# Four halo buffers instead of two, and the next image's plan entered first, in a four-layer image kernel on one core

## The chip, the cores and the metric

The kernel runs on one core of a Trainium2 chip. The metric is the device time of one execution in microseconds. A program is run several times and the median is taken; beside that one execution is profiled, and all durations below come from it.

## The reference

A batch of four images of 64 x 64 pixels with 96 channels passes through four layers. The change lies in the first two, both selective scans over an image (4096 tokens) in four directions:

```
x   -> normalise over groups of channels -> in_proj: 96 -> 192 (inner) and 192 (gate z)
inner -> depthwise 3x3 convolution -> SiLU -> x_tok          gate z -> SiLU -> z_t
for each of 4 directions k (token orders):
    dt, B, C = projections of x_tok[order k]
    h_t = exp(dt*A) * h_(t-1) + dt*x_t*B_t ;  y_k[t] = C_t . h_t
sum over k of weight_k * y_k, brought back to image order, + D * x_tok
-> layer norm -> * z_t -> (layer 0: out_proj 192 -> 96, + x)
```

Layer 0 has diagonal and radial orders, and weights for the four directions that depend on the pixel. Layer 1 has rows and columns, forwards and backwards, and plain sums, and its output goes on into a convolutional feed-forward part. Layers 2 and 3 (attention, FFN, Fourier layers) follow and are not touched.

## The kernel before

Class Stream runs both scan layers as eight batches, one per layer and image, in one order written out by hand (`run`). Each batch is 4 directions x 4 segments of 1024 tokens. A segment is a run of slots in which DVE scans (line 918), POOL multiplies by C (line 928), ACT makes the decays (line 906) and PE spreads and gathers (lines 898 and 939). These stretches are the bulk of the time and are the same in both kernels.

Between two batches stands `side_by_side`. It interleaves two works that don't depend on each other:

- `front(bt)` prepares the batch after the next: it loads the image in four strips of 16 rows (`measure`, line 368, tile da), takes statistics on DVE (line 372), and loads for each strip the row above and the row below (`edges`, line 380, tile halo). `project` clears the border of a padded buffer (line 415, tile spare, two buffers), normalises the strip and its halo rows on DVE (line 420), and multiplies by the input weights on PE (line 428 for the inner half, 444 for the gate), with ACT writing into the padded buffer (line 434) and making z (line 447). `convolve` runs the 3x3 convolution of the strip on PE out of the padded buffer (line 481), SiLU on ACT (493), and transposes (502, 505) into x_tok (514).
- `merge(bt)` ends the batch before: in eight chunks of 512 tokens it loads x_tok (line 557, tile dx, one buffer), multiplies it by D on POOL (565 in layer 0, 568 in layer 1), adds the four directions on DVE (610 in layer 0, 614 in layer 1), where the last two of layer 0 are gathered by POOL's indirect DMAs (587, tile h, four buffers), takes layer-norm statistics (624), and in `finish` normalises (637), transposes on PE into one PSUM buffer u (645), scales on ACT (655), multiplies by z on DVE (659), projects on PE (671) and adds x (676).

At the first boundary `side_by_side` has two fronts and no merge. The six boundaries after that have one front and one merge (four merge layer 0, two merge layer 1), the next has only a merge, and the last stands behind the whole scan.

The order of instructions is decided at build time by a planner, class Plan. Each work is a generator that yields an engine and a cost in microseconds before it emits instructions, or a condition to wait for. The planner always takes the thread with the earliest start, and of equal ones the one with the larger `ahead`, then the one that was entered first:

```
start = max(th.at, self.free.get(th.wants[0], 0.0))
if best is None or (start, -th.ahead) < (best[0], -best[1].ahead):
    best = start, th
```

Fronts are entered with ahead = 1 and merges with 0; threads that a thread enters inherit its value. Buffers of limited number are taken from rings (`take`, `give`): a thread that wants a buffer waits in the plan until another has given one back. `give` counts from the moment at which the using instruction is put into the program, not from its end on the chip; the semaphores that hold the instruction until the buffer is really free are set by the framework. On the chip each engine's instructions run in the order that the planner made. All loads and stores named here are issued by one queue, SP, in that same order.

The halo of a strip is given back at the end of `project`, after the gate's projection:

```
yield from plan.together([outer(j) for j in range(2)])
give(st.x, st.halo)
```

Of the kernel before, what the change touches and what calls it, by code (L numbers as in the profile page):

```python
# [22 lines left out]
HW = 64  # L23
L = HW * HW
C = 96
# [175 lines left out]
class Rings:  # L201
# [9 lines left out]
    def take(self, pool, shape, tag, bufs, dtype=F32):  # L211
        ring = self.rings.setdefault(tag, SimpleNamespace(busy=[False] * bufs, at=0, tiles=None))
        while ring.busy[ring.at]:
            yield lambda: not ring.busy[ring.at]
        slot, ring.at = ring.at, (ring.at + 1) % bufs
        ring.busy[slot] = True
        x = ring.tiles[slot] if ring.tiles else self.k.t(pool, shape, tag, dtype, bufs=bufs)
        self.slots[id(x)] = ring, slot, x
        return x
# [92 lines left out]
class Stream:  # L312
# [38 lines left out]
    def front(self, bt, plan, rings, first=None):  # L351

        k, nc, lay = self.k, self.nc, bt.lay
        take, give = rings.take, rings.give
# [18 lines left out]

        def edges(s, st):

            halo = yield from take(self.tmp, [C, 2, HW], "halo", 2)
            yield "SP", 0.1
            for n, row in enumerate((s * 16 - 1, s * 16 + 16)):
                if 0 <= row < HW:
                    nc.sync.dma_start(halo[:, n], x[:, row * HW : (row + 1) * HW])  # L380
            yield "none", 2.5
            st.halo = halo

        for s, st in enumerate(strips):
            plan.add(edges(s, st))
# [300 lines left out]
    def side_by_side(self, ahead, behind=None, flush=None, seg=None):  # L686


        k, nc = self.k, self.nc
        plan, rings = Plan(), Rings(k)  # L690
        self.ended, self.idle = False, None

        def ending():

            yield "none", 1.2
            if flush:
                flush()
            self.idle = k.t(self.ps_y, [128, CH], "y")
            self.ended = True
            yield "PE", 4.0  # L700

        def fill():
            if self.idle is not None:
                data = self.layers[0].diag.rearrange("p h t c -> p (h t c)")[:, :384]
                nc.tensor.matmul(self.idle[:GC, :384], self.zeros, data, start=True, stop=True)

        def states():

            for at in range(2 * NSG):
                yield "none", 50.0 if at == 0 else 4.0  # L710
                yield "SP", 0.1
                self.load_states(seg, *divmod(at, NSG))
            self.load_dt(seg, 0)

        plan.fill = fill
        if seg:
            plan.add(states())
        if behind:
            plan.add(self.merge(behind, plan, rings))
        for bt in ahead:  # L720
            plan.add(self.front(bt, plan, rings, None if bt is ahead[0] else ahead[0]), 1)
        plan.add(ending())
        plan.run()
        self.idle = None
# [1386 lines left out]
```

## Time and profile before

| | |
|---|---|
| median of 3 runs | 15879.18 us (15832.05 to 15962.23) |
| profiled execution | 15861.73 us |
| its span, first to last instruction | 15859.9 us |
| granted TensorE clock, mean | 0.875 |
| DVE busy | 12867.0 us (81%) |
| POOL busy | 9781.6 us (62%) |
| ACT busy | 8291.1 us (52%) |

The first page of the profile gives busy times and a strip of 40 slices for each engine. A group or timeline line names the time, the duration, the engine, the source line (L), the operation, the tile written and the tile read, the shape, and in square brackets how long the engine was idle before it and what ended that. Tile names leave out the number of the buffer. "SPq" is the issue of a DMA on SP; the data land some microseconds later.

### The profile page before, as it was taken

The numbers are of one execution on the slowest core, as the hardware profiler recorded it, in microseconds if no ns is written. First come the engines' busy times: TensorE is split into PE (matmuls) and PEld (weight loads), VectorE is DVE, ScalarE is ACT, GpSimd is POOL, SyncE is SP. The second block draws the span as 40 slices with busy tenths as digits, with TensorE's granted clock in tenths as the row PEclk, the third lists the DMA queues.
The fourth block names the chain that finished last, engine by engine and source line by source line (L and its number), as shares of the span: only waits on it lengthen the run. The fifth ranks groups of instructions, "written<-read, shape, count | busy, mean of one in ns | idle before, by whom it ended". The sixth has DMA issues, their size and how long they took to land. (4 is left out here: it accounts for less than half of the span.)

```text
span 15859.9 us, 190275 instructions
## 1 busy us (share of the span) xinstructions
PE 13616.6 (86%) x70721; PEld 4897.8 (31%) x70721; DVE 12867.0 (81%) x9642; ACT 8291.1 (52%) x14188; POOL 9781.6 (62%) x4913
## 2 busy tenths in 40 slices
PE   7888888888888888888888888888888889998877
PEld 3222322232223222322222223222222234443344
DVE  1989798979897989799979997999899965665555
ACT  3656465556565655556655655656556522332333
POOL 0788688867886788677757775777677730000223
PEclk8888888888898888888888888888888899998888
DMA  2333433343334333433343334333433310000132
GB/s 71 110 103 121 153 108 104 120 152 106 104 122 153 106 103 120 154 109 115 113 150 118 108 118 147 111 122 116 141 118 108 115 53 18 18 11 14 46 75 70
DMA packets 662747, 1637.10 MB, mean 103 GB/s; under 512 B 102822, under 2 KB 268459, under 8 KB 658044
## 3 DMA queue, kind: packets, MB, share of 16 engines
q1 hardware_dynamic: 624956, 1549.37, 30.9%
q0 software_dynamic: 36864, 75.55, 1.6%
q8 instruction: 560, 9.18, 0.2%
q14 instruction: 367, 3.01, 0.1%
HBM read 1295.03 MB, written 329.58 MB: 102 GB/s over the span
## 5 line engine op out<-in xcount | busy, mean ns | idle before, releaser
L928 POOL TENSOR_TENSOR hc<-h,bc 128x1024 f32<-128x1024 f32 x3072 | 7186.7, 2359 | 2360.7 <-DVE h L918 1949.8
L918 DVE TENSOR_TENSOR_SCAN h<-da,state,t 128x1024 f32<-128x1024 f32 x2304 | 5271.5, 2329 | 11.5 <-ACT da L906 8.7
L939 PE MATMUL y<-hc,gather_y 128*32 128x512 f32 x12288 | 4270.8, 687 | 628.4 <-POOL hc L928 465.1
L911 DVE TENSOR_TENSOR t<-u,bc 128x1024 f32<-128x1024 f32 x3072 | 3601.2, 1218 | 895.2 <-PE u L898 780.8
L906 ACT ACTIVATE da<-dts,L_A_logs 128x1024 f32<-128x1024 f32 x3072 | 3488.0, 1147 | 726.7 <-DMA dts<-dt_dram 444.4
L898 PE MATMUL u<-dtu,spread 32*128 32x512 f32 x3072 | 1879.7, 739 | 369.4 <-DVE t L911 362.9
L962 PE MATMUL y<-L_diag,zeros 96*32 96x256 f32 x5218 | 1736.9, 463 | 0.0
L918 DVE TENSOR_TENSOR_SCAN h<-da,t 128x1024 f32<-128x1024 f32 x768 | 1711.0, 2269 | 13.1 <-ACT da L906 12.5
L939 PEld LDWEIGHTS y<-hc,gather_y 128*32 128x32 f32 x12288 | 800.1, 117 | 2404.0 <-issue 1210.4
L830 PE MATMUL m<-xs,proj 96*128 96x512 f32 (+1 forms) x2048 | 1018.3, 620 | 121.8 <-ACT dt L839 62.7
L867 ACT COPY dt<-m 96x512 f32<-96x512 f32 x512 | 297.1, 580 | 1458.9 <-PE m L862 1458.9
L898 PEld LDWEIGHTS u<-dtu,spread 32*128 32x128 f32 x3072 | 595.1, 214 | 1433.1 <-issue 1117.5
L962 PEld LDWEIGHTS y<-L_diag,zeros 96*32 96x32 f32 x5218 | 617.2, 132 | 1274.9 <-issue 1114.7
L1289 POOL MEMSET padp<- 128x2448 f32 x32 | 68.6, 2143 | 1396.7 <-PE d L1329 1375.5
L1365 DVE SCALAR_TENSOR_TENSOR hcv<-padv,taps,hcv 128x2048 f32<-128x2048 f32 x384 | 902.2, 2350 | 13.4
L1329 PE MATMUL d<-padp,diag 32*32 32x512 f32 x25600 | 885.5, 601 | 2.0 <-ACT hcp L1344 2.0
L822 POOL TENSOR_TENSOR dtu<-sp_z,dtu 96x1024 f32<-96x1024 f32 x256 | 604.4, 2361 | 384.7 <-ACT dtu L820 382.3
L862 PE MATMUL m<-sp_z,ident 96*96 96x512 f32 x1024 | 537.1, 606 | 195.6 <-ACT sp_z L856 195.6
L834 ACT ACTIVATE sp_z<-m,L_dtb 96x512 f32<-96x512 f32 x512 | 349.3, 682 | 540.4 <-PE m L830 531.6
L1329 PEld LDWEIGHTS d<-padp,diag 32*32 32x32 f32 x25600 | 483.4, 103 | 370.6 <-issue 197.7
L986 ACT COPY spare<-m 128x512 f32<-128x512 f32 x384 | 225.6, 587 | 711.0 <-PE m L983 710.8
L830 PEld LDWEIGHTS m<-xs,proj 96*128 96x128 f32 (+1 forms) x2048 | 322.4, 177 | 829.4 <-issue 325.8
(275 smaller groups left out, 15623.6 us busy)
## 6 DMA issues: line engine op xcount, KB each, us to landing
bc<-bc_dram SPq DMA_DIRECT2D x1024, 512.0 KB
dts<-dt_dram SPq DMA_DIRECT2D x768, 512.0 KB
dt_dram<-dt SPq DMA_DIRECT2D x256, 384.0 KB
y_tok<-spare SPq DMA_DIRECT2D x64, 768.0 KB
dt<-y_tok SPq DMA_DIRECT2D x128, 384.0 KB
x_tok<-y_rows SPq DMA_DIRECT2D x32, 768.0 KB
z_t<-z_rows SPq DMA_DIRECT2D x64, 384.0 KB
dx<-x_tok SPq DMA_DIRECT2D x64, 384.0 KB
```

Of the source, the lines that this page charges most:

```text
L822: rest = lambda half: nc.gpsimd.tensor_add(r[:, half], z[:, half], r[:, half])
L830: nc.tensor.matmul(ps, proj[:, src, to], xs[:, src, cols], start=src == 0, stop=src == 1)
L862: nc.tensor.matmul(ps, k.ident[:C, :C], term[:, half, cols], start=at == 0, stop=at == 2)
L898: self.nc.tensor.matmul(seg.u[:, cols], self.spread[rows, :], seg.dtu[rows, half, cols], start=True, stop=True)
L906: self.nc.scalar.activation(da, seg.dts[cb], AF.Exp, scale=seg.bt.lay.neg_a[:, seg.kd, g : g + 1])
L911: self.nc.vector.tensor_mul(gr.t, gr.seg.u, self.bc[:, 0, gr.sg, :])
L918: self.nc.vector.tensor_tensor_scan(gr.h[:, order], gr.da[:, order], gr.t[:, order], start, op0=ALU.mult, op1=ALU.add)
L928: self.nc.gpsimd.tensor_mul(gr.hc, gr.h, self.bc[:, 1, gr.sg, :])
L939: nc.tensor.matmul(seg.y[at : at + GC, :], self.gather_y, gr.hc[:, part * CH : (part + 1) * CH], start=gr.sg == 0, stop=gr.sg == NSG - 1, ...
L962: self.nc.tensor.matmul(gr.seg.y[at : at + GC, :256], self.zeros, gr.seg.bt.lay.diag.rearrange("p h t c -> p (h t c)")[:, :256], start=Fal ...
L1329: nc.tensor.matmul(pc[i][j * 32 : (j + 1) * 32, :], diag[mine, ON_PE.index(t), tap, :], pad[mine, j * 8 + dy : j * 8 + dy + 8, dx : dx + H ...
L1365: nc.vector.scalar_tensor_tensor(to, win, wt, to, op0=ALU.mult, op1=ALU.add)
```

## The change

The ring of halo buffers gets four instead of two, so that the halo rows of all four strips can be loaded at once. And `side_by_side` enters the fronts ahead of the merge.

```diff
@@ front, edges @@
-            halo = yield from take(self.tmp, [C, 2, HW], "halo", 2)
+            halo = yield from take(self.tmp, [C, 2, HW], "halo", 4)
             yield "SP", 0.1
@@ side_by_side @@
         if seg:
             plan.add(states())
+        for bt in ahead:
+            plan.add(self.front(bt, plan, rings, None if bt is ahead[0] else ahead[0]), 1)
         if behind:
             plan.add(self.merge(behind, plan, rings))
-        for bt in ahead:
-            plan.add(self.front(bt, plan, rings, None if bt is ahead[0] else ahead[0]), 1)
         plan.add(ending())
         plan.run()
```

## The prediction

> **What bounds the kernel now.** I read the page first: busy shares, then the 40 slices.
>
> ```profile
> PE 13616.6 (86%) x70721; PEld 4897.8 (31%) x70721; DVE 12867.0 (81%) x9642; ACT 8291.1 (52%) x14188; POOL 9781.6 (62%) x4913
> DVE  1989798979897989799979997999899965665555
> ```
>
> PE and DVE are both busy for most of the span, but the DVE row dips from 9 to 7 at regular places. Those are the stretches between two batches; the scans between them contain nothing that this change touches. The time from the last scan of one batch to the first product of the next, off the DVE timeline, is 178.7, 181.0, 178.6 and 178.9 us for the four boundaries that merge a layer-0 batch, 157.7 and 159.3 us for the two that merge a layer-1 batch while an image is projected, and 102.5 us for the one with no image left, which stays as it is. So 1034 us, 6.5% of the span, is in play, plus the first 190 us, where two images are projected with nothing to merge.
>
> Next, line 420, the normalisation of a strip and its halo rows on DVE: what its engine waited for.
>
> ```profile
> its engine sat idle before it (us, times) until:
>   DMA halo<-in_x: 103.8, 8
>   DMA halo<-x: 81.1, 8
> ```
>
> These are 184.9 us over 16 waits, two for each of eight images. By window, 58.7 lie in the first 300 us and 126.1 in the six boundaries (21.3, 23.8, 22.1, 20.9, 17.5, 20.5). Why the loads are late stands in the timeline of SP at the first boundary:
>
> ```profile
> 1806.46 0.42 SPq L380 DMA_DIRECT2D halo<-in_x  x1
> 1819.73 0.38 SPq L1005 DMA_DIRECT2D y_tok<-spare  x1
> 1820.15 1.31 SPq L380 DMA_DIRECT2D halo<-in_x  x2
> 1821.56 2.22 SPq L368 DMA_DIRECT2D da<-in_x  x4
> 1823.83 0.42 SPq L557 DMA_DIRECT2D dx<-x_tok  x1
> ...
> 1895.24 0.91 SPq L380 DMA_DIRECT2D halo<-in_x  x2
> 1916.22 0.55 SPq L380 DMA_DIRECT2D halo<-in_x  x1
> ```
>
> Two strips' halos and all four strips' images (da) already go ahead of the sums' loads (dx); only strips 2 and 3 wait, for one of two halo buffers, until the projections of strips 0 and 1 give it back. The DVE timeline of the same boundary shows the price:
>
> ```profile
> 1826.33 1.28 DVE L372 BATCH_NORM_STATS2 gn_stats<-da 96x6 f32<-96x512 f32 x2 [13.92 <-DMA da<-in_x]
> 1902.97 1.60 DVE L420 TENSOR_SCALAR halo<-halo,gn 96x128 f32<-96x128 f32 x1 [9.31 <-DMA halo<-in_x]
> 1922.13 0.31 DVE L420 TENSOR_SCALAR halo<-halo,gn 96x64 f32<-96x64 f32 x1 [11.95 <-DMA halo<-in_x]
> 1987.92 0.68 DVE L676 TENSOR_TENSOR x_in<-x_in,u 96x512 f32<-96x512 f32 x1 [2.05 <-PE u L671]
> ```
>
> Last, what else bounds a boundary. POOL issues 64 gathers of the sums (1.25 us each) and eight products (1.8), about 12 us for a chunk, and it is idle only when DVE is:
>
> ```profile
> 1924.03 0.94 POOL L587 DMA_INDIRECT h<-y_tok,scan_inv  x1 [8.02 <-DVE ln_stats L624]
> 1934.89 1.81 POOL L565 TENSOR_TENSOR dx<-dx,sp_z 128x768 f32<-128x768 f32 x1 [6.02 <-DVE ln_stats L624]
> ```
>
> After POOL's last product (1949.3) the end is set by the chain of the last chunks through one PSUM buffer: line 676 runs at 1974.7, 1981.3, 1987.9, one chunk in 6.6 us. And in the first 190 us a wait shows that will matter below, DVE clearing the padded buffer (two of them) for strip 2, while PE convolves strip 0 out of it (ACT reads that result at 138.33):
>
> ```profile
> 138.65 0.12 DVE L415 MEMSET spare<- 96x72 f32 x1 [17.30 <-issue]
> ```
>
> [...] at 1922.13 the halo wait of 11.95 us also holds the sums, and POOL's 8.02 follows from it. [...] the convolution of one strip takes 8.4 us after a full pipe and 11.6 to 12.4 us after gaps, up to 19.8 us in layer 1. [...]
>
> **The change part by part.** The exchange of the two plan.add lines alone leaves every engine's order of instructions as it was: the front already has ahead = 1 against the merge's 0, and in the trace its loads stand before dx already. It costs nothing. The whole change is the halo ring of 4.
>
> SP: three more halo loads (1.31 / 2 = 0.65 us each) go between the y_tok store and the da loads. DVE stands waiting for da then (13.92), so each boundary begins 2.0 us later: 12 us for six, and about 3 us in the first phase, where da of the second image goes behind six halo loads.
>
> DVE: the plan now places strip 2 right behind the sums of chunk 0 and strip 3 inside chunk 2, while before they stood inside chunks 4. The plan takes a padded buffer as free once a convolution has been issued, not when it has ended. So line 415 now meets the wait of 138.65 above. I lay the first boundary's instructions in the new order with their own durations:
> - Chunk 0's statistics end at 1846.9 + 2.0 = 1848.9. Convolution 0 ends at 1858.8 + 2.0 = 1860.8. New stall 11.9, with all sums, and line 637 of chunk 0, queued behind.
> - Strip 2 1.2, chunk 1 8.9 (sums 5.5, normalising 1.5, statistics 1.9): 1870.9. Chunk 2's dx could be loaded only from 1863.4, when chunk 1 freed the one buffer; 7.5 us to land and 1.8 on POOL: 1872.7. Then 5.4 of sums and line 659: 1878.1.
> - PE keeps line 671 of chunk 0 ahead of convolution 1, and it waits for that line 659 (1875.3); with 3.7 for it, convolution 1 starts at about 1879 and, after this gap, takes the 12.4 of the trace: 1891.5. Second stall on the buffer, 13.4. Strip 3 1.3, rest of chunk 2 5.3: 1898.
> - Here all four strips are normalised, at 1898 instead of 1922.4, but three chunks are summed where the old order had four and most of a fifth at 1922. Chunks 3 and 4 at 11 us: 1920, against 1925.5. The sums gain 5 to 6 us, and POOL ends at about 1943.
> - PE: convolutions 2 and 3 start at about 1915 and 1945 and end at 1926 and 1953.5 (before 1920.0 and 1950.3), since lines 645 and 671 of chunks 1 to 3 now stand ahead of them. After convolution 3 one chunk fewer is left: 9.5 for chunk 4, three at 6.6, 3.2 to the first product: 1986 against 1991.1. Gain 5 us; four such boundaries 20 us.
>
> Layer 1 merges have no gathers, and PE sets their end:
>
> ```profile
> 8216.30 0.34 DVE L420 TENSOR_SCALAR halo<-halo,gn 96x128 f32<-96x128 f32 x1 [7.22 <-DMA halo<-x]
> 8233.78 0.31 DVE L420 TENSOR_SCALAR halo<-halo,gn 96x64 f32<-96x64 f32 x1 [10.33 <-DMA halo<-x]
> 8276.04 1.22 DVE L659 TENSOR_TENSOR yt<-yt,xs 96x1024 f32<-96x1024 f32 x1 [15.99 <-ACT yt L655]
> ```
>
> Convolution 3 runs 8254.2 to 8271.2 there, last because strip 3 came late. In the new order convolution 1 starts at about 8190 instead of 8180 (chunk 1's line 645 stands ahead and waits for DVE), convolution 2 at about 8224 as before, but strip 3 is ready, so the 21 us between convolutions 2 and 3 fall to about 14. Gain 7 to 16, I take 10: 20 us for two.
>
> ACT gets 20 more table loads in the whole program (1.28 us a row): 26 us beside PE and DVE work, inside the estimates above. If that cover is gone they cost up to 26.
>
> The first phase: PE is busy 165 of 190 us and strip 2's projection follows its predecessor with no gap (165.46, halo ready at 163.3), so the 58.7 us of halo waits are hidden and return nothing; -3 us as said.
>
> Sum: 20 + 20 - 3 = 37 us. The profiled execution took 15861.7 us (span 15859.9); so 15825. The median of the runs shown is 17 above the profiled one, and their spread is 130 us. Bounds: a layer-0 boundary from 10 worse (the two stalls of 25.3 and the 2.0 against 21 of halo waits, and 4 of table loads) to 16 better (convolutions all at 8.4); layer 1 from 0 to 20; together from 46 slower to 104 faster.
>
> **The rivals.** (1) All halo waits of the boundaries come back: 126 - 15 = 111 faster, 15751. For it: POOL's waits of 8.02 and 6.02 sit right behind them. Against: the buffer wait at 138.65, and the one-chunk chain at the end. (2) Slower: line 415 of strips 2 and 3 is the mechanism, on DVE, at 11.9 + 13.4 a boundary, plus 2.0, less 21.0: 6 us, times six, 38 slower: 15900. It decides if the two buffer waits exceed 19 us a boundary and the lagging sums, not convolution 3, set the end. (3) Nothing: PE holds the end anyway, and only the issue costs stay, 15 slower: 15877. That the change doesn't do what it says is true for its order of loads, as said; the buffers remain.
>
> **How the numbers follow.** The forecast 0.48, (1) 0.20, (2) 0.20, (3) 0.12. About 1% is what a measurement of this kernel can tell from no change, 159 us. More than that in gain is over the 126 us of all halo waits in the boundaries[...]: 0.08. In loss it is 26 us in each boundary, over any price above: 0.05. The range takes the bounds, 15758 to 15908, and the scatter of runs: 15745 to 15915.
>
> **What would show it.** Right: line 420 waits for no halo in the boundaries; line 415 waits 10 us or more, twice a boundary; da lands 2 us later; layer-0 boundaries at 170 to 178 us, layer-1 at 140 to 155; 20 more table loads. Wrong: line 415 hardly waits (then rival 1), or POOL's last product comes later than 137 us after the last scan (rival 2).

## The result, and the profile after

The kernel after takes 15925.45 us (median of 12 runs, 15882.75 to 15953.48). The kernel before, run beside it, takes 15927.19 (12 runs, 15832.05 to 15970.63). The ratio of the runs (not that of the two medians) is 1.0007, 95% interval [0.9994, 1.0021]: no difference that this measurement can tell, and 100 us above the forecast of 15825. A second comparison on another occasion (e5 below) gives 1.0015 [1.0003, 1.0027]. The profiled execution of after took 15950.05 us, its span 15948.3.

Below, convolution n is the 3x3 convolution of strip n, a stretch is the time from the last scan of one batch to the first product of the next, and e1 to e18 are the experiments. These were made in five groups, each on another chip: e1 to e4, e5 to e8, e9 to e11, e12 to e15, e16 to e18. In e1 to e4 and e9 to e11 convolution 0 of every layer-0 stretch took 17 to 35 us in place of 8.4, in the kernel before too, so their layer-0 stretches are read against e1 and not against the first profile (the last section shows this).

The page of after has nearly the same shares as before, and DVE's row keeps its dips; where before showed a single 7 at the second and third boundary, after shows 7 and 8 side by side:

```profile
PE 13682.0 (86%) x70689; PEld 4927.5 (31%) x70689; DVE 12867.5 (81%) x9642; ACT 8313.6 (52%) x14208; POOL 9779.4 (61%) x4913
DVE  0989798978897889899979997999899965665555
```

Line 420 has no wait for a halo left. Line 415, which clears the padded buffer and had only 35.0 us before, all in the first phase, now reads (us, times, by what ended the wait):

```profile
L415 DVE MEMSET spare<- x32: 118/118/118, 120.3 to 9821.2; 96x72 f32 x32
...
its engine sat idle before it (us, times) until:
  PE m L481: 128.6, 11
  issue: 69.5, 4
  PE t L481: 12.4, 1
```

The twelve waits for PE are the six stretches between batches, two in each: 141.0 us, where the halo waits had been 126.1. L481 is the convolution that still reads the buffer. So in the stretches the change replaced one wait by a slightly longer one. In the first phase line 415 waits 69.5 us in place of 35.0, where line 420 had waited 58.7.

Timeline of SP in after at the first boundary that has a merge (start, duration, what ran): five halo loads now go ahead of da, 3.04 us against 1.31 for two.

```profile
1831.78 0.38 SPq L1005 DMA_DIRECT2D y_tok<-spare  x1
1832.20 3.04 SPq L380 DMA_DIRECT2D halo<-in_x  x5
1835.35 1.78 SPq L368 DMA_DIRECT2D da<-in_x  x4
1837.17 0.42 SPq L557 DMA_DIRECT2D dx<-x_tok  x1
```

Timeline of DVE there (in brackets the idle time ahead of the instruction and what ended it). The last scan instruction of the old batch ended at 1824.29:

```profile
1839.19 5.40 DVE L372 BATCH_NORM_STATS2 gn_stats<-da 96x6 f32<-96x512 f32 x8 [14.90 <-DMA da<-in_x]
...
1873.14 0.12 DVE L415 MEMSET spare<- 96x72 f32 x1 [12.40 <-PE t L481]
...
1902.03 0.12 DVE L415 MEMSET spare<- 96x72 f32 x1 [13.98 <-PE m L481]
...
2003.07 0.68 DVE L676 TENSOR_TENSOR x_in<-x_in,u 96x512 f32<-96x512 f32 x1 [2.05 <-PE u L671]
```

All strips are normalised at 1903, 79 us after the last scan in place of 110. The sums gain at first: the statistics of chunk 4 end 106.8 us after the last scan, in place of 113.2. Then they fall behind. Timeline of POOL, its last four products (chunks 4 to 7) in after:

```profile
1917.08 1.80 POOL L565 TENSOR_TENSOR dx<-dx,sp_z 128x768 f32<-128x768 f32 x1 [2.13 <-DMA sp_z<-L_weight_x]
1935.39 1.80 POOL L565 TENSOR_TENSOR dx<-dx,sp_z 128x768 f32<-128x768 f32 x1 [2.87 <-DMA sp_z<-L_weight_x]
1952.64 1.80 POOL L565 TENSOR_TENSOR dx<-dx,sp_z 128x768 f32<-128x768 f32 x1 [3.63 <-DMA sp_z<-L_weight_x]
1969.63 1.80 POOL L565 TENSOR_TENSOR dx<-dx,sp_z 128x768 f32<-128x768 f32 x1 [5.01 <-DMA sp_z<-L_weight_x]
```

They are 18.3, 17.3 and 17.0 us apart, and the last one ends at 1971.4, 147.1 us after the last scan. In the kernel before it ended at 136.9. Timelines of POOL and DVE in before, the products of chunks 5 and 7 and between them the first sum of chunk 5:

```profile
1902.68 1.80 POOL L565 TENSOR_TENSOR dx<-dx,sp_z 128x768 f32<-128x768 f32 x1 [3.90 <-DMA sp_z<-L_weight_x]
...
1926.66 1.40 DVE L610 SCALAR_TENSOR_TENSOR hc<-dt,fuse,dx 128x192 f32<-128x192 f32 x4
...
1947.52 1.83 POOL L565 TENSOR_TENSOR dx<-dx,sp_z 128x768 f32<-128x768 f32 x1
```

There the product of chunk 5 was ready 22 us before DVE took it: in the middle of chunk 4's sums DVE stood at the halos of strips 2 and 3, and POOL went ahead. In after, DVE's stalls come earlier, and it takes each product from chunk 5 on within 2 us of its end, as in chunk 6:

```profile
1954.47 1.41 DVE L610 SCALAR_TENSOR_TENSOR hc<-dt,fuse,dx 128x192 f32<-128x192 f32 x4 [3.30 <-POOL dx L565]
```

From the end of chunk 4's statistics to POOL's last product it is 23.7 to 25.8 us in the four layer-0 stretches of before, and 37.6 to 40.3 in those of after.

In layer 1 the loss is larger. Timeline of ACT in the first of these two stretches (8167.00 to 8341.87): the square root of chunk 1's variance (L632) stands between two SiLUs (L493) of convolution 0's result, and waits for DVE statistics that are queued behind line 415:

```profile
8214.70 0.69 ACT L493 ACTIVATE xc<-t,L_conv_b 128x512 f32<-128x512 f32 x1 [5.73 <-PE t L481]
...
8221.20 0.30 ACT L632 ACTIVATE ln_mv<-ln_mv,eps 128x4 f32<-128x4 f32 x1 [4.51 <-DVE ln_mv L625]
...
8222.81 0.69 ACT L493 ACTIVATE xc<-t,L_conv_b 128x512 f32<-128x512 f32 x1
```

The second SiLU comes 8.1 us after the first; with the next convolution (8249.77 and 8258.23) it is 8.5. PE waits behind each of the two, 4.44 us both times. Timeline of PE:

```profile
8223.55 1.17 PE L428 MATMUL t<-halo,L_in_wT 96*96 96x128 f32 x4 [4.44 <-ACT xc L493]
```

Convolution 2 starts 116.4 us after the last scan (before 98.2) and convolution 3 at 150.0 (before 127.6).

Lengths of the stretches, last scan to first product, off DVE's timeline (before and e7 are two profiles of one order of instructions; so are after and e5, whose orders on DVE, ACT, POOL and SP are the same instruction for instruction):

```
                      merging layer 0                merging layer 1
before            178.7  181.0  178.6  178.9         157.7  159.3
before (e7)       178.2  179.9  177.8  180.7         157.6  158.8
after             181.5  188.0  184.5  180.3         174.9  173.3
after (e5)        187.3  185.8  179.7  183.1         173.0  165.8
```

After minus before is 48.5 us in the first pair; e5 minus e7 is 41.7, and each time the first product of all came later too (398.8 against 389.0, 399.4 against 396.4). The times differ by 0.07% and 0.15%, 11 and 24 us. The rest of the span scatters by more than that: the scan stretches, whose instructions are the same, sum to 11129 us (before), 11157 (after), 11196 (e7) and 11107 (e5). Whether part of the 45 us comes back there, or these profiles drew more than the median run, no run settles.

### The profile page after: what moved, and what is told of

Its sections match the earlier page's. It is cut to its first block, busy times and chain, and to the rows that moved or that the text cites. A ratio compares the mean times of both kernels' runs of the same rounds, so it can differ in the third digit from the quotient of the medians.

```text
span 15948.3 us, 190201 instructions
## 1 busy us (share of the span) xinstructions
PE 13682.0 (86%) x70689; PEld 4927.5 (31%) x70689; DVE 12867.5 (81%) x9642; ACT 8313.6 (52%) x14208; POOL 9779.4 (61%) x4913
## 5 line engine op out<-in xcount | busy, mean ns | idle before, releaser
L1365 DVE SCALAR_TENSOR_TENSOR hcv<-padv,taps,hcv 128x2048 f32<-128x2048 f32 x384 | 902.2, 2350 | 13.4
L822 POOL TENSOR_TENSOR dtu<-sp_z,dtu 96x1024 f32<-96x1024 f32 x256 | 604.0, 2359 | 396.4 <-ACT dtu L820 394.0
```

Source lines behind the costliest of these rows:

```text
L822: rest = lambda half: nc.gpsimd.tensor_add(r[:, half], z[:, half], r[:, half])
L1365: nc.vector.scalar_tensor_tensor(to, win, wt, to, op0=ALU.mult, op1=ALU.add)
```

## Experiments

Theory 1: the waits of line 415, which the plan causes by taking a padded buffer as free when a convolution is issued, replaced the halo waits and are what the change paid with. Theory 2: something behind them sets the end, the loads of the sums on SP, or PE. A third possibility is that the first two profiles differ by chance.

**e1, e7: the kernel before again.** No edit.

> The kernel before, unchanged, as a control for the lengths of the stretches between batches. If these lengths belong to the kernel (both theories below), the four stretches that merge a layer-0 image are within 2 us of 178.7, 181.0, 178.6 and 178.9, the two of layer 1 within 2 us of 157.7 and 159.3, the ratio of the times is 1.000, and the span moves by the scan stretches between them. If the lengths scatter from run to run, they differ from these by 5 us and more, and the 48 us that the kernel after lost there in its profile (2.8, 7.0, 6.0, 1.4, 17.2, 14.0) show nothing.

> The kernel before once more, for the state of this chip beside the two kernels above. If the length of convolution 0 in the layer-0 stretches (8.4 us in the first profile, 27 to 31 in the second) belongs to the chip or the load of a program, it is the same in all kernels of one session, and either near 8.4 or near 28; if it is drawn anew in every execution, the four stretches of one profile mix both.

e1: ratio 1.0002 [0.9989, 1.0015]. Layer 1 158.5 and 161.2, as expected; layer 0 missed by far: 206.1, 202.4, 214.0, 203.7. e7: all six within 2 us of the first profile. Convolution 0 took 27 to 31 us in layer 0 in e1 and 8.4 to 9.2 in e7: it is slow or fast in all layer-0 stretches and all kernels of a group of runs. As every group was made on another chip, the runs cannot tell whether this goes with the chip or with the occasion. The whole times go with it: the medians of before are 16004 and 16029 us beside the two slow groups, and 15895 to 15927 beside the others. Where convolution 0 takes about 8.4 us the lengths repeat, within 2 us for before and e7, within 7.5 for after and e5.

**e5: the halo ring alone**, the two plan.add lines not exchanged (against the kernel before).

```
-            halo = yield from take(self.tmp, [C, 2, HW], "halo", 2)
+            halo = yield from take(self.tmp, [C, 2, HW], "halo", 4)
```

> The kernel before with the halo ring of 4 alone, the two lines of the plan not exchanged (every engine's order is that of the kernel after). Theory 1 (the stalls of line 415 and what they shift cost time): layer-1 stretches at 173 to 175 again, against 158 to 161; the layer-0 stretches longer than those of the kernel before on the same chip by 1 to 8 us each; time 1.001 to 1.004. Theory 2 (the first profiles differed by chance): layer-1 stretches within 3 us of 159, layer-0 ones within 3 us of those of before on this chip; time 1.000.

Ratio 1.0015 [1.0003, 1.0027]; lengths as in the table: layer 0 on average 4.8 us longer than e7, layer 1 15.4 and 7.0 (its 165.8 misses the 173 to 175 expected). Chance is out for the stretches.

**e2, e11, e18: the buffer given back late**, three runs of one kernel.

```
-            give(st.whole)
+            plan.add(give(x) for x in [st.whole])
```

The new thread begins, in the plan's time, when the convolution ends; then the buffer counts as free. DVE's order gets strips 2 and 3 later. So the edit moves two things at once, the wait of line 415 and the place of the strips in DVE's queue.

> The kernel after, with one thing else: the plan takes a padded buffer as free at the planned end of the convolution and not at its issue, so strips 2 and 3 go some 8 us of planned time later into DVE's order. Theory 1, the wait of line 415 for the buffer replaced the halo wait and costs the same: the waits of line 415 for PE (152.4 us with those of the first phase) fall below 40, the layer-0 stretches come back to 170 to 178, those of layer 1 to 150 to 158, time 0.995 to 0.998 of before. Theory 2, what follows sets the end (the loads of dx behind x_in on SP in layer 0, the order on ACT in layer 1): the waits of line 415 go, the stretches stay at 180 to 187 and 172 to 175, time 1.000 to 1.003.

> The kernel after with the padded buffer given back late, once more, to be read where convolution 0 of the layer-0 stretches takes 8.4 us. Theory 1: layer-0 stretches at 170 to 178, waits of line 415 below 6 us each, as in layer 1 (1.3 and 5.8 there, stretches of 152 to 154). Theory 2 (layer 0 waits for the sums' loads): they stay at 180 to 187 though the waits shrink.

> The kernel after with the padded buffer given back late and two padded buffers, a third time, to be read in layer 0 if convolution 0 takes 8.4 us: if the waits of line 415 alone decide, their sum there (25 us in after, 5 to 6 with three buffers) and the stretch (184 and 172.6) move together: waits of 5 to 12 go with 172 to 178. If a stretch of 180 to 187 stands with short waits, the place of the strips in DVE's order matters beside them.

e2: ratio 1.000 [0.9985, 1.0016], where theory 1 expected 0.995 to 0.998 (the 152.4 us of waits for PE in the expectation are 141.0 in the trace). e2 and e11 show a gain in layer 1 alone: 151.9, 153.6 and 148.8, 149.9, with waits of line 415 of 1.3 and 4 to 6. In layer 0 their convolution 0 takes 33 to 34 us, line 415 waits 21 and 13, and they are no shorter than e1 (207 to 219). e18 has 8.4 to 9.0 us there and shows both layers: 176.9, 182.7, 168.1, 167.3 and 150.3, 151.0. Line 415 in e18 (us, times, by what ended the wait; first phase included, to which the 66.2 belong):

```profile
  issue: 66.2, 4
  PE m L481: 16.0, 6
  DMA dx<-x_tok: 1.7, 1
```

141.0 us of waits for PE in the stretches became 16.0, and the six stretches together take 996 us, against 1083 in after and 1034 before. The 182.7 is longer than the 172 to 178 expected, with a wait of only 1.0 us: its last 28 us ran at a granted clock of 0.50, with line 676 every 10.35 us, those of the 168.1 and 167.3 at 1.00, with line 676 every 6.60. POOL's last product, which comes before that tail, is at 132.3 to 134.8 in all four, against 136.9 to 139.2 in before and 140.8 to 148.9 in after and e5. ACT's timeline in the first layer-1 stretch of e18 has the square root ahead of the SiLUs now, and no hole between these:

```profile
8174.67 0.30 ACT L632 ACTIVATE ln_mv<-ln_mv,eps 128x4 f32<-128x4 f32 x1 [3.81 <-DVE ln_mv L625]
...
8177.90 1.27 ACT L493 ACTIVATE xc<-t,L_conv_b 128x512 f32<-128x512 f32 x2 [1.63 <-PE t L481]
8179.05 0.69 ACT L493 ACTIVATE xc<-m,L_conv_b 128x512 f32<-128x512 f32 x1
```

So theory 1 holds in both layers, in layer 0 on one run: the same four halo buffers gain once line 415 does not stand waiting in DVE's queue. The late return by itself gives nothing: e6 below has it in layer 0 too, with two halo buffers, and its stretches there are no shorter than those of before.

**e4, e9, e14: a third padded buffer**, e9 and e14 (one kernel) with the late return as well. The second edit shown makes room for it: the convolution's rows now share three buffers with yc, a tile of the scan.

```
-            whole = yield from take(self.w, [128, 2 * 18 * (HW + 2)], "spare", 2)
+            whole = yield from take(self.w, [128, 2 * 18 * (HW + 2)], "spare", 3)
...
-                xc.append((yield from take(self.tmp, [128, CH], "xc", 3)))
+                xc.append((yield from take(self.tmp, [128, CH], "yc", 3)))
```

> The kernel after, with a third padded buffer; the room for it comes from letting the convolution's rows and the scan's yc share three buffers. Theory 1 (line 415 decides): its waits for PE in the stretches between batches fall from about 25 us each to under 5, both late strips are normalised by 65 us after the last scan in place of 79, the layer-0 stretches fall to 165 to 174, layer 1 to 145 to 156, time 0.993 to 0.997. Theory 2 (what follows decides): the waits go, the stretches stay above 177 and 170, time 0.999 to 1.003.

> The kernel after with a third padded buffer (room as in the run before with three) and with the buffer given back in the plan at the planned end of the convolution: strip 2 needs no wait at all, strip 3 is placed after convolution 0's planned end. Theory 1 (line 415's waits are what the wider halo ring paid with, in layer 0 too): the waits of line 415 between batches fall below 3 us each, convolution 1 of the layer-0 stretches starts at 58 to 62 us after the last scan in place of 64 to 67, and they take 168 to 177 us against 178 to 181 before and 180 to 187 after; layer 1 150 to 156; time 0.996 to 0.998 of before where convolution 0 takes 8.4 us. Theory 2 (in layer 0 the loads of the sums on SP and POOL's queue set the end): no waits on line 415, layer-0 stretches still 180 to 187, layer 1 150 to 156; time 1.000 to 1.001.

> The kernel after with a third padded buffer given back late, once more, if convolution 0 takes 8.4 us here. Theory A (SP's loads): line 415 waits below 3 us each, the layer-0 stretches still 179 to 187. Theory B (line 415's stall pushes PE's chain): convolution 1 at 56 to 61, convolution 3 ends at 130 to 137, stretches of 168 to 177. Layer 1 as before here, 155 to 157.

e4 missed: 1.0040 [1.0026, 1.0054], slower. The third buffer serves strip 2, and strip 3 moves up to the place where strip 2 stood and waits there for convolution 0: 11.7 and 12.0 us in layer 1, 30 in layer 0. One wait a stretch is left of two. Why the whole got slower is not shown; its scan stretches, which now share yc's buffers, are 31 us longer than e1's too. e9: 1.0010 [0.9992, 1.0027], layer 1 155.4 and 157.5, convolution 0 of layer 0 at 26 to 32 us. e14 has 8.4 us there, and layer 0 at 173.9, 172.9, 171.5, 172.2. Timeline of DVE and of POOL in its first stretch (last scan ended at 1815.47):

```profile
1861.12 0.12 DVE L415 MEMSET spare<- 96x72 f32 x1 [2.68 <-PE m L481]
...
1985.99 0.68 DVE L676 TENSOR_TENSOR x_in<-x_in,u 96x512 f32<-96x512 f32 x1 [2.05 <-PE u L671]
```

```profile
1947.19 1.80 POOL L565 TENSOR_TENSOR dx<-dx,sp_z 128x768 f32<-128x768 f32 x1 [6.84 <-DMA sp_z<-L_weight_x]
```

One wait of 2.68 in place of 12.40 and 13.98; POOL's last product ends at 133.5 in place of 147.1. Convolution 3 starts at 116.6 (after 133.6). Layer 1 is 158.6 and 158.3 though line 415 waits less than 2 us there: no better than before, where e18 has 150. There both late strips are normalised by 50 us, in e18 line 415 clears for them at 47 and 71. So the place of the strips in DVE's queue seems to count in layer 1 beside the wait; no run moves it alone.

**e3, e10, e13: two buffers for x_in and dx; e12: for x_in alone** (the second edit only). The order of DVE and ACT is that of after; with two dx buffers POOL's products move one chunk ahead of its gathers.

```
-            x = yield from take(tmp, [128, T, DI], "dx", 1)
+            x = yield from take(tmp, [128, T, DI], "dx", 2)
...
-                plan.add(load(("x", n), tmp, [C, CH], "x_in", 1, lay.x_in[:, bt.b, cols_of(n)]))
+                plan.add(load(("x", n), tmp, [C, CH], "x_in", 2, lay.x_in[:, bt.b, cols_of(n)]))
```

> The kernel after, with two buffers for x_in and two for dx in place of one each, so that no load on SP waits for a store of x_in and a chunk's dx is fetched one chunk ahead; the order of PE, DVE and ACT stays. Theory 1 (line 415 decides): the stretches stay within 3 us of 181.5, 188.0, 184.5, 180.3, 174.9, 173.3, time 1.001. Theory 2 (loads of the sums decide): chunks 4 to 7 of a layer-0 merge follow each other in 11 to 13 us in place of 16 to 17, POOL's last product comes 125 to 135 us after the last scan in place of 147, the layer-0 stretches fall to 168 to 176, layer 1 moves by less than 5, time 0.996 to 0.998.

> The kernel after with two buffers each for x_in and dx once more, to be read where convolution 0 of the layer-0 stretches takes 8.4 us. Theory 1 (line 415 decides): layer-0 stretches at 180 to 187 as in the kernel after. Theory 2 (the sums' loads decide): POOL's last product at 125 to 138 us after the last scan in place of 141 to 149, the stretches at 168 to 177.

> The kernel after with two buffers for x_in, nothing else; only SP's order moves (a load of x_in no longer stands behind the store from the same buffer). Theory A (in the layer-0 stretches the sums lag because SP's queue stands 8 to 9 us behind x_in's store, four times a stretch, ahead of the loads of dx): SP's wait of line 536 for the store falls from 137 to 141 us to under 20, POOL's last product comes at 128 to 138 us after the last scan in place of 141 to 149, the layer-0 stretches fall from 180 to 187 to 173 to 179. Theory B (the chain of PE behind the first stall of line 415 sets the end): SP's wait goes, convolution 3 still ends at 137 to 142, the stretches stay at 180 to 187. Read where convolution 0 takes 8.4 us.

> The kernel after with two buffers each for x_in and dx, a third time, if convolution 0 takes 8.4 us here. Theory A: POOL's last product at 120 to 135, stretches of 168 to 177; theory B: 180 to 187.

SP's own waits show why this was worth a run: line 536, the load of x_in, waits for the store from the same buffer, and holds all loads behind it. After, then e12 (us in total, times, the longest):

```profile
SPq L536 <- DMA x<-x_in: 140.6, 28, 10.9
```

```profile
SPq L536 <- DMA x<-x_in: 9.7, 8, 1.7
```

(92.9 before.) With that wait gone POOL's last product comes at 137.5 to 139.9 in e12, in place of 140.8 to 148.9, so the wait did hold the sums. In e13, where the products run ahead, the last one comes at 124.2 to 129.2, inside the 120 to 135 expected, and POOL's last gather ends at 136.4 to 140.9. The stretches stay: 185.2, 179.7, 188.2, 187.8 (e12), 188.3, 189.3, 190.2, 180.3 (e13). Behind the sums comes the chain of the last chunks through one PSUM buffer, which runs at two speeds. Timeline of PE near the end of the first stretch, after and then e12:

```profile
1994.48 1.96 PE L671 MATMUL u<-yt,out_w 96*96 96x512 f32 x4 [0.73 <-DVE yt L659]
1997.22 1.08 PE L645 MATMUL u<-ident,hc 128*96 128x128 f32 x8 [0.78 <-DVE x_in L676]
...
2001.08 1.96 PE L671 MATMUL u<-yt,out_w 96*96 96x512 f32 x4 [0.73 <-DVE yt L659]
```

```profile
2003.30 3.73 PE L671 MATMUL u<-yt,out_w 96*96 96x512 f32 x4
2007.80 1.94 PE L645 MATMUL u<-ident,hc 128*96 128x128 f32 x8 [0.78 <-DVE x_in L676]
...
2013.65 3.73 PE L671 MATMUL u<-yt,out_w 96*96 96x512 f32 x4
```

A chunk takes 6.6 us in one and 10.35 in the other; the granted clock of the last 28 us around these lines is 1.00 and 0.54. Three of four stretches of e12 end at the slow rate. By estimate that costs three chunks times 3.75, 11 us, and eats what the loads gave. The one that does not, the second, took 179.7 us against 188.0 in after. The same groups of matmuls take 3.73 us in e12 and 1.96 in after (line 671), 1.94 and 1.08 (line 645). What keeps the clock low in this tail no run shows: PE is busy for 23.2 of those 28 us in e12, and in after for 19.8 of the last 28, at 1.00. e3 gave 1.0006 [0.9992, 1.0019]; in e3 and e10 convolution 0 is slow, and they say nothing on layer 0. So neither theory wins alone here: the loads do hold POOL, and taking their wait away moved the end in one stretch of e12 only.

**e6: layer 1 alone**: the kernel before with four halo buffers only where a layer-1 image is merged, and with the late return of e2 everywhere.

```
+            halo = yield from take(self.tmp, [C, 2, HW], *(("halo4", 4) if plan.plain else ("halo", 2)))
...
+        plan.fill, plan.plain = fill, behind and not behind.lay.ordered
...
```

> The kernel before, where only the stretches that merge a layer-1 image get four halo buffers, and where the plan gives a padded buffer back at the planned end of the convolution (the order in all other stretches is that of before). Theory 1 (in layer 1 the halo waits were worth something, and line 415 took it away): the two layer-1 stretches take 150 to 155 us against 158 to 161, line 415 waits below 7 us in each place there, the layer-0 stretches are those of before; 12 to 16 us less in all, time 0.999. Theory 2 (PE sets the end of layer 1 whatever DVE does): 157 to 162, time 1.000.

150.9 and 151.8, as theory 1 had it, layer 0 180.2, 183.6, 179.7, 179.9; the time 1.0004 [0.9985, 1.0022] cannot show 14 us.

**e8: SP's loads kept out of convolution 0** (before, with a wait in the plan ahead of the loads of chunk 2 and later, until the rows of strip 0's convolution are stored). One of its five lines:

```
+            yield lambda: n < 2 or plan.stored
...
```

> The kernel before, where in the layer-0 stretches SP's loads for the sums of chunk 2 and later and for line 659 and 676 wait in the plan until the rows of strip 0's convolution have been stored, so that SP's loads leave convolution 0 alone; POOL's gathers stay. If the DMA bursts starve PE of issue in convolution 0, it takes 8 to 9 us here where the kernel before shows 27 to 31 on the same chip; if not, it stays as there. The sums start 10 to 15 us late for this, so no gain in time is expected where convolution 0 takes 8.4 us anyway.

No answer: convolution 0 took 8.4 us, but so it did in before on that occasion (e7). That loads keep PE from issuing was the author's guess, and is not shown. The hold costs 9.5 us a layer-0 stretch against e7 (191.0, 191.2, 182.3, 190.0).

**e15 to e17: the parts put together.** e15 is e6 with two buffers for x_in. e16 has four halo buffers where a batch is merged, the late return, and three padded buffers in layer 0. e17 is e16 with two buffers for x_in, cut from an idle tile.

```
+        plan.fill, plan.room, plan.halos = fill, 3 if behind and behind.lay.ordered else 2, 4 if behind else 2
...
+            yield lambda: plan.room; plan.room -= 1; whole = yield from take(self.w, [128, 2 * 18 * (HW + 2)], "spare", 3)
...
+            plan.add(freed(x) for x in [st.whole])
...
```

> The candidate: the order of before in layer 0, four halo buffers and the late return of the padded buffer in layer 1 alone, and two buffers for x_in. If the loads of x_in also hold the sums in the order of before (SP's wait of line 536 is 92 us there), the layer-0 stretches fall from 178 to 181 to 174 to 178, layer 1 takes 150 to 153, time 0.998 of before; if not, layer 0 stays and the time is 0.999.

> What the runs point to: four halo buffers where a batch is merged (two in the first phase), the padded buffer given back in the plan at the planned end of the convolution, and three padded buffers where a layer-0 image is merged, two where a layer-1 image is. The stretches should be those seen apart: 171 to 174 us in layer 0 (before 178 to 181) and 149 to 154 in layer 1 (before 158 to 161), about 42 us less in all, time 0.997 of before; where convolution 0 takes 27 to 31 us in layer 0 the gain there may go, and 0.999 is left.

> The kernel of e16 with two buffers for x_in as well, cut out of a dts tile that lies idle there. If the loads of x_in (waits of 8 to 9 us of line 676 in the run with three late buffers) hold the end once line 415 is gone, the layer-0 stretches fall from 172 to 165 to 170 and the time to 0.996; if the last chunks' chain through one PSUM buffer holds it, they stay at 171 to 174, time 0.997.

```
       time against before           layer 0                        layer 1        POOL's last product, layer 0
e15    0.9977 [0.9965, 0.9989]   177.2  181.5  176.3  174.8      150.7  149.2      134.1 to 140.4
e16    0.9965 [0.9953, 0.9978]   172.6  173.7  174.1  171.7      158.4  158.4      134.2 to 134.9
e17    0.9964 [0.9951, 0.9977]   170.1  169.9  170.2  168.8      152.7  158.5      129.2 to 130.0
```

All three beat the kernel before, e16 and e17 by 0.35% (15827.85 and 15836.50 against 15895.60), and so by inference the kernel after, which was not run beside them. With line 415's wait down to 2 to 4 us a stretch the loads of x_in do shorten the layer-0 stretches: by 3.3 us each between e16 and e17, at the weak end of what was expected. The times of the two do not differ. The miss of e16 and e17 is layer 1: 158.4 where 149 to 154 was expected. The limit of two buffers there did not keep strip 3 back; line 415 clears for both late strips side by side at 46 and 47 us and waits less than 0.5, and convolution 3 runs slow (16.9 us, in e18 12.4, at granted clocks of 0.64 and 0.68). The place of the strips does not settle it: e17 has them there too, and its first layer-1 stretch took 152.7. The stretch of convolution 3 in e16 (length, busy times of PE, PEld, DVE, ACT and POOL, granted clock, DMA share, GB/s):

```profile
8239.00:8257.00 18.00, 13.98 (x222) 6.09 (x221) 2.65 (x6) 4.07 (x8) 0.00 (x0) 0.64 0.34 111
```

A version with e17's layer 0 and e18's layer 1 would be the next one; it was not run.

## Why the prediction was wrong, by its own steps

- **The exchange costs nothing.** Right: e5 without it has the lengths of after and the same ratio within its interval.
- **SP, 2.0 us a boundary.** Half: five halo loads take 3.04 us as counted, but DVE's wait for da grew by 0.6 to 1.2 us in layer 0 (13.92 to 14.90) and 1.4 to 1.7 in layer 1. For the first phase 3 us were forecast; the first product of all came 9.8 and 3.0 later.
- **The halo waits vanish, line 415 takes their place.** Right in kind and size: 11.9 and 13.4 forecast, 12.40 and 13.98 in the first boundary, 12.05 and 11.38 in layer 1. Convolution 1 took 12.10 against 12.4; all strips were ready at 79 us against 86.
- **Chunks 3 and 4 at 11 us, and the gain of 5 to 6 us handed on to POOL, done at 131 us.** The first half was right: chunk 4's statistics end at 106.8 us (103.2 to 108.6 over the four) against 107.6 forecast and 113.2 to 114.6 before. The second half is the step that failed in layer 0. POOL ends at 141 to 149. The forecast took over the 24 us that lie between these two points in before, but there POOL had a product in store, made while DVE stood at the halos of strips 2 and 3. After the change DVE does not stand there, and the traces show no product in store: 38 to 40 us in place of 24 to 26. SP's wait for x_in is part of that (e12, without it, has 34); what makes up the rest no run separates.
- **Convolution 3 ends at 141, then 32.5 us to the end.** The first half was right (142.0); the tail took 39.6. In before the end lies 40 to 43 us behind POOL's last product and 41 behind convolution 3, which does not tell which of them sets it. In e14, e16 and e17 it keeps its distance from the product (36 to 41) while that from convolution 3 grows (41 to 49), so the end seems to go with the product; in stretches that end with a chunk every 10.35 us (e12, e18) it is 45 to 50 behind the product. Forecast 5 us gained in each of four, measured 1.4 to 7.0 lost.
- **Layer 1, 10 us gained in each of two.** That PE sets the end there fits the traces: it lies 13 us behind convolution 3 in before and in after. Two terms failed. Convolution 1 came as forecast (63.5 against 63 us), convolution 2 not "as before": 116.4 against 98. The forecast followed DVE and PE, and left out ACT's queue: line 632 stands there between two SiLUs, which run 8.1 and 8.5 us apart as it waits 4.51 and 4.86 us for DVE's statistics, and so DVE's stall is handed on to PE, which waits 4.44 us behind each of the two, once ahead of convolution 1 and once ahead of convolution 2. Convolution 1's delay of 10 us, which the forecast let a slack take up, stayed, and 8 more came on behind it (33.2 us to convolution 2 in place of 24.9). And the gap between convolutions 2 and 3 did not fall from 21 us to 14 though strip 3 was ready: it was 22.4 and 19.9, and 21 in e18 too. Measured 17.2 and 14.0 lost.
- **20 more table loads at nothing.** Their number was right (364 to 384, each of 1.28 us). Their 26 us are not to be told apart in the stretches.
- **The base.** 15861.7 was the profiled execution of before; the median of the 12 runs beside after is 65 us above it, and that of e5's comparison 34. With the right base the forecast gain of 37 would have given 15890, still a gain that was not there.
- **Readings and sums.** The 19.8 us of a convolution in layer 1 hold a pause of 7.3 us behind its first 16 matmuls; the others took 11.4 us, at a granted clock of 0.69. In the first boundary of before the four convolutions took 8.40, 12.38, 11.62 and 8.40 us at a granted clock of 1.00, 0.67, 0.72 and 1.00, and PE was busy for 9.2, 6.9, 6.7 and 8.6 of the 10 us ahead of each. That fits the forecast's reading of gaps, but that the gaps lower the clock was the author's inference; no run tests it. The bounds do not quite add up: four times 10 and the 3 of the first phase are 43 slower, not 46, and the 104 faster leave these 3 out.

Rival 2 was the one that happened: both waits together above 19 us a boundary (26.4 in the first, 19.8 at the least) and POOL's last product later than 137 us, the sign that the prediction had named for it. That sign was weak, as before itself has 136.9 to 139.2. The rival gave 38 us slower; the stretches lost 42 to 48, the time 11 to 24 (the 11 inside the scatter). Its chance of 0.20 was too low, and the forecast's 0.48 rested on a gain of one engine handed on unchanged to the next.

## What to carry to other kernels

When a wait for a buffer is taken away, look for the next ring on the same path and ask when its buffer is really free: a planner that gives a buffer back when its last reader is issued can move the consumer up into a wait in front of everything else in its queue, as line 415 was here (12.40 and 13.98 us in the first boundary). One line that gives the buffer back at the reader's planned end turned 48 us lost in the stretches into 38 gained (996 us in e18, one run, against 1034 before). A stall of one engine can be the time in which another works ahead, as POOL did here (its product lay ready for 22 us): before a gain is handed on from one engine to the next, look in the trace how long the products lay ready before they were taken. And follow a stall through every queue it feeds, as here from DVE through ACT (4.51 us) to PE (4.44 us), before a cover is called free.

## What the runs showed of the hardware

In e1 to e4 and e9 to e11 the convolutions of the layer-0 stretches, above all the first, took up to four times as long for the same matmuls (x219 of PE in both views, 216 of them of line 481). Convolution 0 of the first stretch in e1, then in the first profile of before (columns as in the view of e16 above):

```profile
1863.00:1893.00 30.00, 28.25 (x219) 7.67 (x218) 9.95 (x27) 2.94 (x4) 21.44 (x21) 0.66 0.68 190
```

```profile
1850.00:1859.00 9.00, 9.00 (x219) 5.42 (x218) 5.59 (x19) 2.90 (x4) 6.87 (x8) 1.00 0.85 257
```

The granted clock, 0.66 against 1.00, would by itself make about 13 us of the 8.4, by an estimate from these two views (8.4 divided by 0.66). The timeline of weight loads in e1 shows more: few at a time, with holes that nothing in the profile explains ("issue").

```profile
1866.78 0.16 PEld L481 LDWEIGHTS m<-spare,L_diag 32*32 32x32 f32 x3 [1.31 <-issue]
1868.21 0.13 PEld L481 LDWEIGHTS t<-spare,L_diag 32*32 32x32 f32 x2 [1.27 <-issue]
1868.93 0.10 PEld L481 LDWEIGHTS t<-spare,L_diag 32*32 32x32 f32 x1 [0.59 <-issue]
1869.65 0.18 PEld L481 LDWEIGHTS t<-spare,L_diag 32*32 32x32 f32 x3 [0.61 <-issue]
```

The holes lie where the DMA engines are fullest (share 0.99 to 1.02 in slices of 4 us at 1864 to 1872 and at 1880), and in the layer-1 stretches of the same runs, which have no gathers, convolution 0 takes 8.4 to 9.9 us. Yet a share of 1.03 at 1854 did no harm in the first profile, so DMA load alone is not enough. The cause stays open. It adds about 27 us to each layer-0 stretch of before (206.5 against 179.3 on average), and a gain in layer 0 can vanish under it: e2's layer-0 stretches were 4.5 us longer than e1's, where the same kernel in e18 was 5.5 us shorter than before.

The other surprise is the scatter of what nobody touched: the scan stretches of one order of instructions sum to anything from 11107 to 11196 us. So the time of a single profiled execution is no base for a forecast of some tens of us, while the length of a stretch between two batches repeats within 2 us in before (e7) and within 7.5 in after (e5).
